# The second feed-forward product of a fused graph layer, computed in two halves of 128 output columns

## The chip, the cores and the metric

The kernel runs on one core of one Trainium2 chip. The metric is the device time of one execution in microseconds. The profile is one execution taken by the hardware profiler; its times are counted from the start of its span.

## The reference

There are 64 graphs of 256 nodes with 256 features, all in 32-bit floats. Each graph goes through two layers of attention over an adjacency matrix. The part that matters here is the end of the first layer: a layer normalisation, a feed-forward block with 1024 hidden columns, and a second normalisation.

```
x  = _ln(src + attn_out, g1, beta1)                 # [256, 256] for one graph
ff = gelu(x @ W1 + b1, approximate=False) @ W2 + b2 # [256, 1024] @ [1024, 256]
x  = _ln(x + ff, g2, beta2)
```

The second product, `gelu(...) @ W2`, is the one that is changed.

## The kernel before

One graph is a program of some hundred operations, written by `program(g)`. Each operation names its engine, what it reads and what it writes. The function `in_order` sorts the operations of all 64 graphs by a due time: the graph's number times `PERIOD` (50.00) plus the entry of the operation in `STARTS`. The first four graphs and some at the end have lists of their own, `FIRST` and `LAST`. The due times set only the order in which each engine takes its instructions; semaphores do the rest. Work of several graphs is so interleaved that TensorE always finds a matmul of some graph whose inputs are ready.

The work of one graph on TensorE, by the names in the profile, is: `pq`, `pk`, `pva` (projections), `s` (scores, four heads side by side in 32 rows each), `po` (attention times values, four heads side by side in 32 columns each), `pwo`, then `ph` (`x @ W1`, line 717), `pw` (the product with W2, line 735; also `pwo`, `pwa`, `pwb` of line 364 are matrix products of the same size of tile), and the projections of the second layer. In the first two and the last three graphs TensorE also makes transposes `py` and `po` at line 412; elsewhere these are made by another way.

The hidden activations `hT` lie as eight chunks of 128 hidden columns on the partitions, each with 256 nodes. For the second product, `emit_w2` takes for each half `t` of the nodes the eight chunks in turn: a 128x128 piece of `hT` is the stationary operand (loaded as weights) and the chunk of `w2` with all its 256 output columns is the moving operand. Eight matmuls add up in one half of the PSUM tile `pw2`; there are 16 for a graph. Four operations of two matmuls each are written per half `t`. A 32-bit matmul leaves two records of a weight load and two of a matmul in the trace, so a graph shows 32 of each at line 735 and the whole kernel 2048.

After `pw2` is complete, VectorE adds the residual in place (`add_dve`, line 442), takes statistics, normalises into `y1`, and hands on to the second layer.

Of the kernel before, what the change touches and what calls it, by code (L numbers as in the profile page):

```python
# [23 lines left out]
P = 128  # L24
# [21 lines left out]
def in_order(programs, starts, period, first, last):  # L46
# [4 lines left out]
    for g, p in enumerate(programs):  # L51
# [61 lines left out]
    "pw2#4": 140.62, "pw2#5": 141.02, "pw2#6": 141.41, "pw2#7": 148.05, "pw2#8": 148.44, "pw2#9": 148.83,  # L113
    "mv1": 151.17, "rs1": 152.34, "y1": 152.73, "y1b": 153.12, "x2": 157.03, "y1d": 160.16, "y1r": 160.55,
    "y1T": 165.62, "pk1": 168.36, "pq1": 169.92, "k1": 173.05, "q1": 175.39, "s100": 176.17, "e10/0": 179.30,
    "m10/1": 179.69, "e10/1": 180.08, "x2#2": 180.47, "m10/0": 181.64, "s110": 182.42, "m11/1": 182.81,
    "e10/1#2": 183.59, "m11/0": 186.33, "e11/0": 186.72, "pv1": 187.50, "v1": 187.89, "pwb": 188.28,
    "e11/1": 189.06, "e10/0#2": 191.80, "e11/0#2": 192.19, "e11/0#3": 193.75, "e11/1#2": 194.92, "e10/1#3": 195.31,
    "es11/0": 196.88, "zb": 197.27, "es10/1": 199.22, "e11/1#3": 200.00, "e10/0#3": 200.39, "es11/1": 200.78,
    "es10/0": 203.52, "po11": 204.69, "rd11": 205.08, "DVE:po11": 205.86, "po10": 207.81, "rd10": 208.20,  # L120
    "o1/1": 208.59, "o1/0": 212.50, "o1b": 212.89, "DVE:po10": 214.84, "pwa": 220.70, "o1d": 221.48, "o1r": 221.88,
    "mv2": 224.61, "rs2": 225.00, "pwa#2": 225.78, "mv3": 226.56, "rs3": 230.86, "y2": 231.25, "y2#2": 234.77,
    "y2#3": 235.16, "SP:y2": 245.70,
# [3 lines left out]
        -15695.655, -15149.395, -14793.414, -14575.593, -14576.679, -12389.4, -12473.121, -12768.633, -12325.705,  # L127
        -12962.633, -13646.112, -13920.766, -15032.506, -13982.705, -12245.782, -14367.9, -13407.27, -13364.314,
        -12295.865, -12278.788, -15117.887, -14534.961, -14147.504, -13724.315, -11168.884, -13648.66, -14956.242,
        -13925.311, -14243.822, -12844.486, -12674.163, -12439.242, -12618.202, -11646.197, -12711.361, -12646.602,  # L130
        -12660.005, -12483.679, -12536.223, -12670.679, -12672.041, -12540.947, -12616.664, -11428.13, -11287.329,
        -10559.998, -11327.61, -12104.073, -11981.91, -11451.573, -11390.504, -11925.878, -11920.644, -11949.974,
        -11934.31, -11218.912, -10721.604, -10477.164, -10272.81, -9911.323, -10046.084, -10003.332, -10003.33,
        -9888.664, -9828.572, -9137.591, -9093.292, -9361.474, -8629.104, -8880.603, -8662.925, -8385.643, -7361.835,
        -8390.399, -7992.367, -8899.947, -8751.386, -5428.043, -5165.028, -4818.157, -4818.155, -4676.943, -4605.749,
        -4416.199, -4343.259, -4285.804, -4281.04, -4239.384, -4213.9, -4213.898, -4184.711, -4179.417, -4120.528,
        -4116.71, -3848.303, -4082.576, -3952.079, -2701.19, -2573.78, -3544.133, -3351.674, -3835.864, -3735.264,
        -3368.002, -3295.807, -3198.79, -2449.601, -3771.22, -3786.52, -3591.972, -3579.658, -3043.106, -1795.518,
        -1513.493, -1500.436, -1651.414, -3219.503, -3097.003, -3058.447, -2754.345, -2674.088, -2325.015, -2665.857,
        -2767.649, -2502.329, -2296.094, -2078.474, -1848.912, -1820.665, -1784.337, -1810.803, -1497.873, -1460.302,  # L140
        -1376.277, -1486.102, -1312.035, -1183.27, -1105.604, -874.684, -688.763, -640.73, -479.139,
# [3 lines left out]
        -10275.79, -10222.682, -9516.48, -9944.344, -9446.908, -10225.155, -10205.062, -10225.153, -8955.48,  # L145
        -10029.465, -10140.425, -10210.028, -9873.068, -9835.535, -7377.261, -7180.288, -6824.629, -6777.573,
        -9204.865, -8944.093, -8767.724, -8328.16, -8466.442, -9151.761, -8929.815, -8096.162, -7584.68, -6703.905,
        -6451.399, -6098.908, -6444.96, -5961.777, -5877.676, -5160.502, -5109.467, -5086.245, -4692.889, -4420.43,
        -4163.756, -3604.27, -4281.353, -4268.9, -4351.895, -4326.041, -4245.629, -4209.422, -4083.279, -3835.868,
        -2477.164, -2455.124, -2262.278, -2252.074, -2126.011, -2126.009, -2085.054, -2084.485, -2082.849, -2082.237,  # L150
        -2003.412, -1980.986, -1933.415, -1872.594, -1896.355, -1270.113, -1738.724, -1639.29, -1717.421, -1448.705,
        -776.375, -412.725, -842.647, -287.979, -1280.266, -1198.698, -1128.404, -879.237, 70.142, 87.941, -1136.295,
        -1072.342, -1027.743, -460.056, -179.507, 204.948, 210.505, 214.846, 206.412, -1047.223, -408.661, -642.116,
        -358.078, -181.938, -6.862, 30.096, -722.148, 194.821, 209.783, 217.042, 218.303, 226.289, 226.571, 225.524,
        231.48, 237.007, 256.247, 254.861, 257.812, 257.814, 258.162, 258.552, 259.758, 267.688, 288.409,
    ],
    [
        -6647.961, -6937.505, -7329.132, -7090.883, -7287.519, -6750.27, -6499.303, -6250.569, -6335.205, -6198.913,
        -4279.455, -4146.698, -4153.953, -4099.89, -5252.176, -4800.331, -4823.206, -3892.413, -4287.653, -5235.477,
        -4590.983, -4178.05, -5112.062, -3844.17, -3597.583, -3566.893, -3768.04, -4350.565, -4222.211, -4264.419,  # L160
        -4242.206, -3964.02, -4253.173, -4122.444, -4100.627, -4124.943, -3655.64, -3398.956, -3375.271, -3623.161,
        -3199.162, -2900.972, -2887.075, -2770.539, -2607.594, -2602.901, -2418.216, -2218.326, -2198.868, -2082.801,
        -1408.588, -2023.294, -1984.958, -2089.338, -2021.294, -1995.304, -1910.877, -1467.289, -1186.368, -333.252,
        -267.616, -156.633, 7.424, 76.774, 123.113, 123.368, 139.873, 149.02, 149.022, 149.024, 149.026, 159.236,
        168.958, 168.96, 168.962, 222.92, 287.196, 168.964, 170.479, 171.914, 173.278, 205.329, 207.947, 216.563,
        216.861, 176.494, 177.744, 178.409, 187.359, 208.634, 208.636, 180.981, 177.968, 180.983, 202.563, 202.565,
        208.638, 210.695, 212.315, 212.986, 181.086, 197.943, 188.886, 202.77, 209.238, 210.706, 194.919, 188.65,
        208.636, 208.638, 211.76, 218.917, 222.164, 222.166, 219.427, 223.473, 223.475, 233.005, 233.712, 233.714,
        233.362, 238.879, 243.498, 247.259, 248.724, 262.721, 289.372, 289.374,
    ],  # L170
    [
        -3461.383, -4284.528, -4612.308, -2804.152, -2140.617, -2122.888, -3258.861, -2978.606, -3119.93, -2972.723,
        -2165.719, -2120.695, -3398.916, -3131.95, -2419.282, -2394.817, -2186.356, -1899.734, -1900.194, -2312.452,
        -2003.4, -1753.187, -1779.463, -1249.761, -944.255, -944.079, -1047.498, -1911.55, -1631.466, -1637.536,
        -1299.479, -1521.291, -1834.945, -1597.607, -1397.96, -1539.304, -1196.6, -726.368, -580.763, -925.785,
        -509.463, -334.77, -263.148, -168.005, 59.328, 85.165, 104.993, 105.438, 108.842, 124.159, 143.944, 114.717,
        116.225, 124.453, 131.56, 146.986, 151.077, 133.857, 141.768, 155.476, 157.111, 158.347, 158.349, 158.351,
        158.353, 158.355, 158.357, 158.359, 159.116, 160.017, 160.115, 166.361, 167.109, 167.489, 168.742, 198.814,
        212.043, 169.653, 171.471, 169.448, 170.399, 204.058, 205.83, 182.958, 193.225, 175.454, 175.456, 178.467,
        187.187, 190.053, 191.779, 175.456, 178.907, 185.152, 200.986, 202.931, 210.134, 210.136, 211.221, 210.28,  # L180
        179.858, 188.999, 196.052, 198.766, 201.471, 204.23, 186.917, 189.993, 190.152, 198.004, 198.313, 210.696,
        211.816, 211.98, 210.698, 212.107, 220.203, 223.572, 224.434, 224.499, 221.504, 228.418, 228.42, 228.869,
        230.221, 257.27, 257.272, 263.277,
# [3 lines left out]
    [  # L187
        23.519, 13.207, 1.964, 57.459, 95.091, 64.105, 53.036, 55.397, 49.54, 52.235, 66.882, 69.681, 63.952, 67.444,
        63.253, 63.255, 67.027, 67.029, 64.134, 63.255, 63.255, 69.248, 68.931, 79.084, 85.684, 85.957, 87.538,
        67.348, 67.35, 69.834, 69.836, 72.036, 67.35, 72.729, 72.731, 78.757, 78.759, 85.365, 85.367, 85.396, 89.037,  # L190
        89.756, 89.769, 93.049, 96.238, 96.554, 106.07, 109.692, 109.694, 115.731, 126.316, 142.48, 143.083, 141.755,
        141.757, 116.193, 116.195, 111.062, 115.098, 150.04, 150.042, 150.753, 151.373, 151.375, 151.377, 151.59,
        151.592, 151.594, 153.406, 153.408, 153.41, 153.412, 156.132, 156.134, 162.974, 184.129, 313.3, 231.961,
# [47 lines left out]
def fast_path(nc, tc, a, out, bad):  # L241
# [11 lines left out]
    FC = FF // P  # L253

    with ExitStack() as ctx:
# [64 lines left out]
        def program(g):  # L320
# [4 lines left out]
            def T(name):  # L325
                return at_(g, name)
# [417 lines left out]
            y1r = turn("y1")  # L744
# [443 lines left out]
```

## Time and profile before

| | |
|---|---|
| time, median of 3 runs | 2811.23 us (2809.66 to 2811.77) |
| span of the profiled execution | 2809.7 us |
| TensorE matmul, busy | 2785.5 us, 21112 records |
| TensorE weight load, busy | 2090.4 us, 21112 records |
| VectorE / ScalarE / GpSimd, busy | 2070.7 / 1939.3 / 1988.5 us |
| second feed-forward product (line 735), busy | 453.4 us, 2048 records |
| mean granted TensorE clock | 0.997 |

The profile does not give the profiled execution's whole time apart from its span. The span equals the fastest of the three runs to 0.1 us, and the slowest is 2.1 us longer, so that is the room for what lies around it.

A row of the groups gives line, engine, operation, output and inputs, shape, count, then busy time in us and mean duration of one in ns. `PE` is the matmul side of TensorE and `PEld` its weight loads, which run beside the matmuls. [...] records of consecutive matmuls overlap: the pace of a stream is read from the time that a run of records takes in the chain or on the timeline, and not from the mean duration.

### The profile page before, as it was taken

How to read it: one execution, taken by the hardware profiler on the slowest of the kernel's cores; microseconds unless marked ns; L12 is line 12 of the kernel's file. 1: busy time of each engine (PE TensorE's matmuls, PEld its weight loads, DVE VectorE, ACT ScalarE, POOL GpSimd, SP SyncE). 2: the span in 40 equal slices, each digit the busy share in tenths (PEclk: the TensorE clock that was granted, in tenths of full speed). 3: DMA queues.
4: the chain of work that ended last, by engine and by line, in shares of the span. 5: the costliest groups of instructions: out<-in, count | busy, mean ns of one | idle time of the engine just before them, and what ended most of it. 6: DMA issues, size and time to landing. Idle time of an engine off the chain costs nothing.

```text
span 2809.7 us, 54277 instructions
## 1 busy us (share of the span) xinstructions
PE 2785.5 (99%) x21112; PEld 2090.4 (74%) x21112; DVE 2070.7 (74%) x3857; ACT 1939.3 (69%) x3131; POOL 1988.5 (71%) x1526
## 2 busy tenths in 40 slices
PE   9999999999999999999999999999999999999997
PEld 7777777777777777777777777777777777777775
DVE  5667777777777777777777777777777777777776
ACT  5766766767767667677676676776766767767663
POOL 3668767677676686776766867768668677677773
PEclk9999999999999999999999999999999999999999
DMA  3012222122222221212222212122222121221100
GB/s 132 23 47 68 59 70 61 53 72 58 60 68 58 64 61 53 75 58 58 68 61 61 63 52 76 57 58 69 60 61 65 50 76 58 56 83 48 53 27 13
DMA packets 269750, 169.55 MB, mean 60 GB/s; under 512 B 18608, under 2 KB 268976, under 8 KB 269488
## 3 DMA queue, kind: packets, MB, share of 16 engines
q1 hardware_dynamic: 269216, 165.76, 20.5%
q8 instruction: 169, 2.77, 0.4%
q14 instruction: 93, 0.76, 0.1%
q10 hardware_dynamic: 272, 0.26, 0.0%
HBM read 102.77 MB, written 63.18 MB: 59 GB/s over the span
## 4 chain that ended last, share of the span: by engine, by line
PE 97%; DVE 2%; ACT 0%; POOL 0%; issue 0%; DMA 0%; SPq 0%; DVEq 0%; POOLq 0%; ACTq 0%
PE ph L717 16%; PE pw L735 16%; PE po L524 12%; PE s L485 10%; PE pk L350 8%; PE pva L669 8%; PE pq L350 8%; PE pv L364 4%; PE po L531 4%; PE pwo L364 4%; PE pwa L364 4%; PE pwb L364 4%; DVE rd L540 1%; ACT e L501 0%; DVE e L510 0%
## 5 line engine op out<-in xcount | busy, mean ns | idle before, releaser
L558 POOL TENSOR_TENSOR es<-e 128x512 f32<-128x512 f32 x504 | 637.3, 1275 | 580.7 <-issue 441.3
L769 POOL TENSOR_TENSOR e<-e,m 128x1024 f32<-128x1024 f32 x252 | 595.2, 2374 | 105.0 <-DVE e L510 97.8
L540 DVE RECIPROCAL rd<-po 128x256 f32<-128x256 f32 x256 | 440.1, 1737 | 41.3 <-PE po L531 41.3
L717 PE MATMUL ph<-y0T,w 128*128 128x256 f32 x2048 | 466.7, 380 | 1.1 <-ACT y0T L431 0.7
L735 PE MATMUL pw<-w,hT 128*128 128x256 f32 x2048 | 453.4, 379 | 0.0
L717 PEld LDWEIGHTS ph<-y0T,w 128*128 128x128 f32 x2048 | 389.1, 191 | 83.0 <-issue 17.4
L501 ACT ACTIVATE e<-e 128x1024 f32<-128x1024 f32 x256 | 268.5, 1050 | 262.1 <-POOL e L769 261.2
L735 PEld LDWEIGHTS pw<-w,hT 128*128 128x128 f32 x2048 | 388.8, 190 | 53.8 <-issue 1.1
L510 DVE TENSOR_TENSOR m<-s,neg 128x1024 f32<-128x1024 f32 x256 | 311.0, 1216 | 109.0 <-ACT e L501 82.2
L501 ACT ACTIVATE e<-s 128x1024 f32<-128x1024 f32 x256 | 261.0, 1022 | 173.2 <-DVE m L510 96.1
L510 DVE TENSOR_TENSOR e<-s,neg 128x1024 f32<-128x1024 f32 x256 | 304.8, 1214 | 15.8 <-PE s L485 8.1
L765 ACT ACTIVATE m<-s 128x1024 f32<-128x1024 f32 x252 | 252.0, 1026 | 67.1 <-PE s L485 38.9
L485 PE MATMUL s<-q,k 32*128 32x256 f32 x4096 | 294.6, 400 | 0.7 <-ACT q L563 0.7
L485 PEld LDWEIGHTS s<-q,k 32*128 32x128 f32 x4096 | 185.5, 184 | 127.1 <-issue 51.9
L524 PE MATMUL po<-e,v 128*32 128x256 f32 x4096 | 271.9, 383 | 4.1 <-ACT v L563 3.0
L501 ACT ACTIVATE m<-m 128x1024 f32<-128x1024 f32 x256 | 265.3, 1069 | 1.6 <-DVE m L510 1.5
L461 POOL TENSOR_TENSOR rs<-ve,neg_half 128x2 f32<-128x2 f32 x256 | 179.9, 703 | 94.8 <-DVE ve L456 86.8
L669 PE MATMUL pva<-wv,xT 128*128 128x512 f32 x512 | 246.4, 604 | 0.4 <-PE s L485 0.4
L501 ACT ACT_TABLE_LOAD x127 | 162.9, 1283 | 87.9 <-PE s L485 86.7
L724 ACT ACTIVATE hT<-ph,cols 128x256 f32<-128x256 f32 x512 | 209.3, 476 | 20.4 <-PE ph L717 18.8
L677 DVE TENSOR_TENSOR v<-pva,rows 128x512 f32<-128x512 f32 x128 | 87.3, 683 | 170.3 <-PE pva L669 170.2
L524 PEld LDWEIGHTS po<-e,v 128*32 128x32 f32 x4096 | 119.9, 110 | 113.3 <-issue 41.8
(107 smaller groups left out, 4652.5 us busy)
## 6 DMA issues: line engine op xcount, KB each, us to landing
xT<-xT_dram SPq DMA_DIRECT2D x64, 256.0 KB, 3.2
x<-x_dram SPq DMA_DIRECT2D x64, 256.0 KB, 3.0
adj<-adjT_dram SPq DMA_DIRECT2D x64, 256.0 KB, 3.7
out_dram<-y SPq DMA_DIRECT2D x64, 256.0 KB, 2.2
y0d<-y0b SPq DMA_DIRECT2D x236, 64.0 KB, 1.8
y0r<-y0d SPq DMA_DIRECT2D x59, 256.0 KB, 2.8
y1d<-y1b SPq DMA_DIRECT2D x236, 64.0 KB, 1.8
y1r<-y1d SPq DMA_DIRECT2D x59, 256.0 KB, 2.8
```

Of the source, the lines that this page charges most:

```text
L350: nc.tensor.matmul(pt[:, o, :], lhsT=w[:, c, o * P : (o + 1) * P], rhs=s[:, c, :], start=(c == 0), stop=(c == KC - 1),)
L364: nc.tensor.matmul(pt[:, t, :], lhsT=T(s)[:, c, t * P : (t + 1) * P], rhs=w, start=(n == 0), stop=(n == len(parts) - 1),)
L485: nc.tensor.matmul(s[j // 2][:, j % 2, c, :], lhsT=kT[r, hg, c * P : (c + 1) * P], rhs=qT[r, hg, :], start=True, stop=True,)
L501: nc.scalar.activation(T(dst)[:, j], s, AF.Exp, scale=scale, **kw)
L510: lambda: nc.vector.tensor_tensor(T(dst)[:, j], T(src), T("neg")[:, None].to_broadcast([P, 2, NT, D]), ALU.add),
L524: nc.tensor.matmul(po[j * DH : (j + 1) * DH, 0, :], lhsT=v(c, j), rhs=T(e)[:, j, c, :], start=(n == 0 and c == 0), stop=(n == len(parts) - ...
L540: op("DVE", [po], [f"{rd}:rd"], lambda: nc.vector.reciprocal(T(rd), T(po)[:, 1, :]))
L558: lambda: on.tensor_tensor(T(dst)[:, j], T(e)[:, j, 0, :], T(e)[:, j, 1, :], ALU.add),
L669: nc.tensor.matmul(pv.rearrange("p r d -> p (r d)"), lhsT=s[:, c, t * P : (t + 1) * P], rhs=wv0[:, c].rearrange("p r d -> p (r d)"), start ...
L717: nc.tensor.matmul(ph[:, i, :], lhsT=w1[:, c, (f + i) * P : (f + i + 1) * P], rhs=s[:, c, :], start=(c == 0), stop=(c == KC - 1),)
L735: nc.tensor.matmul(T("pw2")[:, t, :], lhsT=T("hT")[:, f + i, t * P : (t + 1) * P], rhs=w2[:, f + i, :], start=(f + i == 0), stop=(f + i == ...
L769: nc.gpsimd.tensor_tensor(T(f"e1{hg}")[:, j], T(f"e1{hg}")[:, j], T(f"m1{hg}")[:, j], ALU.add)
```

## The change

Each half `t` of the second product is made in two halves `h` of 128 output columns. For each `h` the eight chunks of `hT` are taken again as weights, and the moving operand is half a chunk of `w2`, 128 columns. So 16 matmuls of 256 columns per graph become 32 of 128 columns. The same products are added in the same places of `pw2`. The due times get eight more entries per graph, which repeat neighbouring values.

```
             for t in range(NT):
-                for f in range(0, FC, 2):
-
-                    def emit_w2(t=t, f=f):
-                        for i in range(2):
-                            nc.tensor.matmul(
-                                T("pw2")[:, t, :], lhsT=T("hT")[:, f + i, t * P : (t + 1) * P], rhs=w2[:, f + i, :],
-                                start=(f + i == 0), stop=(f + i == FC - 1),
-                            )
-
-                    op("PE", [f"hT/{f}", "c_w2"], ["pw2:g"], emit_w2)
+                for h in range(2):
+                    for f in range(0, FC, 2):
+
+                        def emit_w2(t=t, f=f, m=slice(h * P, (h + 1) * P)):
+                            for i in range(2):
+                                nc.tensor.matmul(
+                                    T("pw2")[:, t, m], lhsT=T("hT")[:, f + i, t * P : (t + 1) * P], rhs=w2[:, f + i, m],
+                                    start=(f + i == 0), stop=(f + i == FC - 1),
+                                )
+
+                        op("PE", [f"hT/{f}", "c_w2"], ["pw2:g"], emit_w2)
...
-    "pw2#4": 140.62, "pw2#5": 141.02, "pw2#6": 141.41, "pw2#7": 148.05, "pw2#8": 148.44, "pw2#9": 148.83,
+    "pw2#4": 140.62, "pw2#5": 140.62, "pw2#6": 140.62, "pw2#7": 140.62, "pw2#8": 140.62, "pw2#9": 141.02,
+    "pw2#10": 141.41, "pw2#11": 148.05, "pw2#12": 148.44, "pw2#13": 148.44, "pw2#14": 148.44, "pw2#15": 148.44,
+    "pw2#16": 148.44, "pw2#17": 148.83, "mv1": 151.17, "rs1": 152.34, "y1": 152.73, "y1b": 153.12, "x2": 157.03,
...
```

The lists `FIRST` and `LAST` change in the same way.

## The prediction

> **What bounds the kernel now.** I read the busy shares first, then the chain of work that ended last, then the groups at line 735.
>
> ```profile
> PE 2785.5 (99%) x21112; PEld 2090.4 (74%) x21112; DVE 2070.7 (74%) x3857; ACT 1939.3 (69%) x3131; POOL 1988.5 (71%) x1526
> ...
> PE 97%; DVE 2%; ACT 0%; POOL 0%; issue 0%; DMA 0%; SPq 0%; DVEq 0%; POOLq 0%; ACTq 0%
> ...
> L735 PE MATMUL pw<-w,hT 128*128 128x256 f32 x2048 | 453.4, 379 | 0.0
> ...
> L735 PEld LDWEIGHTS pw<-w,hT 128*128 128x128 f32 x2048 | 388.8, 190 | 53.8 <-issue 1.1
> ```
>
> TensorE's matmul side is busy 99% of the span and makes up 97% of the chain, so what lengthens its stream lengthens the kernel. The list of waits shows no wait of TensorE at all between 500 and 2000 us. The changed product stands in that stream with no idle time before its matmuls (0.0). Its weight loads, 190 ns each, fit beside matmuls and still leave 53.8 us in which the loading side is idle: before, weights cost nothing here. The chain in order of time gives the pace:
>
> ```profile
> 1384.95 1.73 PE pwo L364 x8
> 1386.68 6.91 PE pw L735 x32
> 1393.59 0.43 PE pk L350 x2
> ```
>
> The 32 records of a graph take 6.91 us with nothing between them, 215.9 ns a record. The next graph's 32 begin at 1429.82, 43.14 us later, and so on through the steady part.
>
> [...] The `pva` records of 512 columns start 0.43 us apart,[...] when nothing runs before it, a 128x128 load lets its matmul start some 104 ns later (below), and in the steady part loads lie under the previous matmul. [...] the question is which ends last.
>
> **The change part by part.** Removed: 2048 records of 256 columns, 2048 x 215.9 ns = 442.2 us of PE stream. Added: 4096 records of 128 columns, each behind its own load. No semaphore wait is added: the only operand waited for is `hT`, as before, and the order of the other engines' instructions, POOL's and SP's queues included, is the same in the built kernel. On TensorE the 32 stay together where the 16 were; in graphs 0, 1 and a few at the ends they are cut at the same places or, with the repeated due times, a few matmuls later. VectorE's add at line 442 starts after the last `pw` record as before and so shifts with it; PE has no wait on it in the steady part, since everything behind it on PE shifts by the same amount. All that is to be priced is the pace of a 128-column record with its own load. The steady part of before has none; I bound it from three places.
>
> First, the matmul itself. The transposes at line 412 are 128-column 32-bit records, each with a load:
>
> ```profile
> 2797.10 0.42 PEld L412 LDWEIGHTS po<-ident,o 128*128 128x128 f32 x4
> 2797.10 0.66 PE L412 MATMUL po<-ident,o 128*128 128x128 f32 x4
> ```
>
> The first of such a run has a record of about 329 ns, as the longest of that line does; three more take 0.66 - 0.33 = 0.33 us, 109 to 110 ns each. [...] so the matmul side alone gives 4096 x 109.2 = 447.3 us, +5.1 us. Their loads, 140 ns long, are shorter than those of ordinary weights, so this is a lower bound: the loading side may be later, not earlier.
>
> Second, the nine warm-up matmuls of 128 columns with ordinary weights. [...]
>
> ```profile
> 3.91 1.06 PE L861 MATMUL warm<-mean_w,ones 128*128 128x128 f32 x4
> ```
>
> Each record there is 421 ns, so (1.06 - 0.421) / 3 = 213 ns a record[...], although a load's record there is 333 ns (median of the line). Loads do follow one another faster than their records are long; 190 ns is no pace, and 4096 x 190 is ruled out.
>
> Third, and deciding: ordinary 128x128 loads under a 128-column record at full clock. They occur where a normal matmul follows a transpose, here `pw` itself near 60.5 us:
>
> ```profile
> L412 PE MATMUL py<-ident,y 128*128 128x128 f32 x3 | 0.5, 273 | 0.0
> L735 PE MATMUL pw<-w,hT 128*128 128x256 f32 x1 | 0.4, 382 | 0.0
> ...
> L735 PEld LDWEIGHTS pw<-w,hT 128*128 128x128 f32 x2 | 0.3, 191 | 0.0
> ```
>
> The `pw` record begins 109 ns after the last transpose's and lasts 382 ns where 379 is usual, and the same 382 stands in all seven places of this kind that I looked up (`pw`, `ph`, `pwa`). I read the 3 ns as waiting for weights: begun 1 to 2 ns after the transpose's matmul, the load was ready about 110 ns later, 112 ns from matmul to matmul. A second reading supports it: an exposed first load of `ph`
>
> ```profile
> 35.88 0.30 PEld L717 LDWEIGHTS ph<-y0T,w 128*128 128x128 f32 x2 [0.89 <-ACT y0T L431]
> 35.88 0.48 PE L717 MATMUL ph<-y0T,w 128*128 128x256 f32 x1 [0.66 <-ACT y0T L431]
> ```
>
> holds its matmul for 483 - 379 = 104 ns and its own record (186 ns) ends some 80 ns after that matmul truly starts. A load under a running matmul ends 190 + 2 ns after that matmul's start; 80 ns earlier is 112. So I take 112 ns: 4096 x 112 = 458.8 us, +16.6 us. All of it lies on the path, because PE has nothing else in its way: 0.26 us more per graph.
>
> Below, I do not go under 109.2 by much, as PE's own transposes show it. Above, 113 (one ns of reading on each load) gives 462.8 us, +20.6.
>
> Issuing costs nothing I can find: the `s` records (64 in 4.3 us of a graph, as many loads) show PE taking an instruction every 34 ns, and the new stream needs one every 56. The instruction queue moves 2.77 MB, 0.4% of the DMA engines; 4096 more records of the 54277 add 8% to that.
>
> Against the profiled span, 2809.7 + 16.6 = 2826.3 us; the median of the runs is 1.5 us above that span, which gives 2827.8.
>
> **The rivals.** A: the loads bind at 112 ns, +16.6 us, 2827.8 (0.60, the forecast; with 111 to 113 as its own range, 2823.7 to 2831.9).
>
> B: the loads stay hidden, because the 3 ns belong to the switch from transposing to multiplying and not to the load. Then the matmul side alone decides, 109.2 ns, +5.1 us, 2816.3: 0.18%, not slower by what can be told. For it: [...] an exposed load is ready after 104 ns. Against it: in one place the load after a transpose began 8 ns late and the matmul waited 5 ns, not 3, which a fixed switch cost would not do. [...] Chance 0.13.
>
> C: in between. At the same seven places the next load starts 110 ns after the one before (two loads fill 0.30 us, and the second is 192 ns); if that is the loads' own pace, 4096 x 110 = 450.6 us, +8.4 us, 2819.6. Chance 0.18.
>
> D: [...] the granted clock gives way: at 116 ns, +32.9 us, 2844. The page shows PEclk at 9 in all slices, and nothing in the trace asks for it. Chance 0.06.
>
> E: faster. [...] The transposes speak against it. Chance 0.03. That the change does not do what it says is excluded by the built kernel, which has 32 matmuls of 128 columns at this place.
>
> **How the numbers follow.** About 0.2% (5.6 us) is what a measurement of this kernel can tell from no change. Slower by more: A, C and D, 0.84. Within: B, and the smaller part of E, 0.14. Faster: 0.02. The range reaches from just under B to just over 113 ns a record: 2815.5 to 2833.
>
> **What would show it.** In the profile after, line 744 should have 4096 records, the chain should show `pw` with 64 records in about 7.17 us (7.0 for B, 7.04 for C), the period of a graph should be 43.40 us, and the matmul records of `pw` should be longer than the 273 ns that a 128-column record takes without waiting, by some 3 ns. Weight loading should be near full under `pw`. A wait of PE on another engine in the steady part, or other lines that take more than before, would make the working wrong, not only its size.

## The result, and the profile after

The changed kernel takes 2828.65 us (median of 3 runs, 2827.53 to 2831.84) against 2811.23: ratio 1.0064, interval 1.0045 to 1.0084. That is 17.4 us slower, 0.8 us from the forecast. The profiled execution is the slowest of the three: 2831.84 us, with a span of 2830.0. So the whole time is 1.8 us above the span, and the profile stands 3.2 us above the median. This matters below. In every execution of these kernels for which both figures are known the difference is 1.7 to 1.9 us. The span of 2809.7 us before therefore belongs to an execution of about 2811.5 us, near the median; that it equals the fastest of the three runs is a coincidence.

The page of the kernel after, busy shares, chain and the two groups of the changed line (744 now):

```profile
PE 2801.9 (99%) x23160; PEld 2160.4 (76%) x23160; DVE 2071.4 (73%) x3857; ACT 1940.0 (69%) x3131; POOL 1988.8 (70%) x1526
...
PE 95%; DVE 2%; ACT 1%; DMA 1%; POOL 1%; issue 0%; SPq 0%; DVEq 0%; POOLq 0%; ACTq 0%
...
L744 PEld LDWEIGHTS pw<-w,hT 128*128 128x128 f32 x4096 | 467.7, 192 | 4.4 <-issue 1.1
...
L744 PE MATMUL pw<-w,hT 128*128 128x128 f32 x4096 | 468.6, 275 | 0.0
```

The loading side, which had 53.8 us of idle time before its loads of this product, has 4.4 now: under `pw` it is full. On the chain TensorE's share has fallen from 97 to 95%, and DMA, ScalarE and GpSimd show 1% each, which the pace of `pw` doesn't explain. The chain of the kernel after in order of time (start, length, what):

```profile
1391.73 1.73 PE pwo L372 x8
1393.46 7.14 PE pw L744 x64
1400.61 1.73 PE pk L358 x8
```

64 records take 7.14 us where 32 took 6.91, and the neighbours keep their 1.73 and stay without gaps. The next `pw` starts at 1436.84, 43.38 us later (43.14 before). The records of line 744 between 500 and 2000 us, duration in ns as least, median and longest:

```profile
L744 PEld LDWEIGHTS pw<-w,hT x2176: 190/192/192, 525.5 to 1964.1; 128*128 128x128 f32 x198
L744 PE MATMUL pw<-w,hT x2176: 272/275/275, 525.7 to 1964.2; 128*128 128x128 f32 x198
```

A 128-column record that doesn't wait is 272 to 273 ns long (the transposes before the change). Nearly all are 275: each waits some 2.5 ns. In the records' own starts, 2642 of the intervals inside `pw` are 112 ns and 1319 are 111, so the pace is 111.7 ns. The transposes before, whose loads are shorter (140 ns), follow one another after 109 ns (27 intervals) or 110 (8), 109.2 on the mean; I take that for the pace of a 128-column matmul alone.

Where the 20.3 us between the two spans lie follows from the starts of `pw` in both traces. Up to `pw` of graph 3: 180.32 against 180.26, +0.1. From there to `pw` of graph 60: 2470.92 against 2457.24, +13.7, which is 57 x 0.240. From there to the end: 178.75 against 172.20, +6.5, of which four graphs of 0.24 make 1.0. The prediction had no term for the other 5.5.

The +0.1 at the start is a sum of opposite parts. Three split products lie in it, 0.7 by the pace, but the profile before also has a stretch of 3.4 us at half clock (a granted clock of 0.50 from 36.7 to 40.1 us), which the profile after lacks. Such a stretch near 36 to 38 us comes in eight of the fourteen profiles of both kernels and all experiments, and `pw` of graph 3 starts anywhere between 178.3 and 182.7 us in the twelve profiles whose `pw` records keep one of the two paces above.

The longer end shows first as 2.9 us in which TensorE is idle, near 2680 us. Tiles that have to be transposed go out to memory in four transfers of 64 KB and come back turned. `o1d` is the outward one for the attention output of the second layer, `o1r` the way back, and `y1d` and `y0d` are outward ones of the same kind. In the first profile after, the last of four `o1d` lands 3.57 us after its issue; in the profile before it takes 1.8.

### The profile page after: what moved, and what is told of

Read it like the earlier page. It is cut to its first block, busy times and chain, and to the rows that moved or that the text cites. A ratio compares the mean times of both kernels' runs of the same rounds, so it can differ in the third digit from the quotient of the medians.

```text
span 2830.0 us, 58376 instructions
## 1 busy us (share of the span) xinstructions
PE 2801.9 (99%) x23160; PEld 2160.4 (76%) x23160; DVE 2071.4 (73%) x3857; ACT 1940.0 (69%) x3131; POOL 1988.8 (70%) x1526
## 3 DMA queue, kind: packets, MB, share of 16 engines
q1 hardware_dynamic: 269216, 165.76, 20.4%
q8 instruction: 185, 3.03, 0.5%
## 4 chain that ended last, share of the span: by engine, by line
PE 95%; DVE 2%; ACT 1%; DMA 1%; POOL 1%; issue 0%; SPq 0%; DVEq 0%; POOLq 0%; ACTq 0%
PE pw L744 16%; PE ph L725 15%; PE po L532 12%; PE s L493 9%; PE pk L358 8%; PE pva L677 8%; PE pq L358 8%; PE pv L372 4%; PE po L539 4%; PE pwo L372 4%; PE pwa L372 4%; PE pwb L372 4%; DVE rd L548 1%; ACT e L509 0%; POOL e L778 0%
## 5 line engine op out<-in xcount | busy, mean ns | idle before, releaser
L744 PEld LDWEIGHTS pw<-w,hT 128*128 128x128 f32 x4096 | 467.7, 192 | 4.4 <-issue 1.1
L744 PE MATMUL pw<-w,hT 128*128 128x128 f32 x4096 | 468.6, 275 | 0.0
L774 ACT ACTIVATE m<-s 128x1024 f32<-128x1024 f32 x252 | 251.8, 1025 | 68.4 <-PE s L493 38.8
L469 POOL TENSOR_TENSOR rs<-ve,neg_half 128x2 f32<-128x2 f32 x256 | 180.1, 703 | 111.7 <-DVE ve L464 104.4
```

Source lines behind the costliest of these rows:

```text
L744: nc.tensor.matmul(T("pw2")[:, t, m], lhsT=T("hT")[:, f + i, t * P : (t + 1) * P], rhs=w2[:, f + i, m], start=(f + i == 0), stop=(f + i == ...
```

## The experiments

Two questions are left: is it the weight load that sets 111.7 ns, and what lengthens the last four graphs. Theory and rival of each run are in its expectation. Times of one group stand beside the runs of before on the same chip.

**The changed kernel again** (`e0_after`, no edit).

> The changed kernel once more, to see which part of its first profile belongs to the change. Theory (a weight load under a 128-column matmul sets the pace, 111.7 ns a record): 64 graphs x (64 x 111.7 - 32 x 215.8 ns) = +15.5 us, so 2826 to 2828 us against a before of 2811, and a period of 43.38 us. The late landing of o1d near the end of the first profile (3.57 us, TensorE idle 2.9 us, then slow for some us) is chance: this profile should not have it, and its span should be about 2826. Rival: the end of the kernel is upset by the change itself, then the idle time of some 3 us before ph near 2680 us comes again in the same place.

2830.23 us (5 runs, 2828.08 to 2833.86) against 2810.19: 1.0077 (1.0063 to 1.0091). The period is 43.377 us again. The profile has no late `o1d`, and its span is 2826.3 as expected, but it is of the fastest of the five runs. The median is above the expectation, so the runs lose more than the pace explains.

**Quarters of 64 columns** (`e1_quarters`).

```
-  w2[:, f + i, :]      # 256 columns, 8 chunks
+  for at, width in cuts[n]:                     # (0,64), (64,64), (128,64), (192,64)
+      m = slice(at, at + width)
+      for f in range(FC):  ... T("pw2")[:, t, m] ... rhs=w2[:, f, m]
```

> The second product in four quarters of 64 columns, each with its own loads: 8192 records. Theory (load sets the pace): [...] the load keeps 108 to 112 ns, so 128 records take 13.9 to 14.3 us a graph and the kernel gains 447 to 473 us: 3258 to 3285. Rival (the 111.7 ns are a matmul of 128 columns[...]): 58.3 ns a record, 477.6 us in all, +36 us: about 2847.

3283.64 us (2 runs) against 2810.19, +473: the load's pace. The chain of that kernel:

```profile
1361.99 14.24 PE pw L738 x128
...
1412.52 14.24 PE pw L738 x128
```

The columns per record are halved again and the interval stays at 111 to 112 ns, so the matmul's width has no part in it. The matmul of 64 columns alone is an estimate of some 56 ns: the paces of 256 and 128 columns, 215.8 and 109.2, are 106.6 apart, and half of that comes off 109.2. The rival's 58 ns a record come from 111.7 in the same way; its 36 us are excluded. The load also keeps 111.7 ns under that short matmul, and does not fall to the 108 ns after which the next load follows an exposed one (35.880 and 35.988 us in the trace before). A limit on how fast TensorE takes instructions is no explanation either: the `s` records, each with a load of its own, follow one another every 67 ns on the mean in the same trace (16 in 1.08 us).

**192 and 64 columns in turn** (`e2_192_64`).

```
+  for m in (slice(0, 192), slice(192, 256)):
+      nc.tensor.matmul(T("pw2")[:, t, m], ..., rhs=w2[:, f + i, m], start=True, stop=True)
```

> Pieces of 192 and of 64 columns in turn, so as many records and columns as in the changed kernel; nothing is accumulated (each matmul overwrites), so that the output is only that of the last chunk. Theory (a load starts only when the matmul before it starts, and takes some 110 ns): 162.5 ns after a 192-column record, 111.7 ns after a 64-column one, 64 records in 8.77 us a graph, +1.87 us a graph, +119 us: about 2930. Rival (loads run further ahead and average out over wide and narrow records): 111.7 ns on the mean, +15 us: about 2827.

2932.52 us (2 runs) against 2810.19, +122. The chain of that kernel, and its matmuls between 500 and 2000 us by shape (busy us, mean ns):

```profile
1353.75 8.72 PE pw L736 x64
1398.75 8.72 PE pw L736 x64
```

```profile
L736 PE MATMUL pw<-w,hT 128*128 128x192 f32 x1083 | 293.0, 352 | 0.0
L736 PE MATMUL pw<-w,hT 128*128 128x64 f32 x1084 | 179.3, 247 | 0.0
```

As many records and columns as in the changed kernel cost 45.00 us a graph, +1.87, as worked out. A record that waits for weights begins before its columns move (382 ns long instead of 326 for a wide one, 275 instead of 219 for a narrow one), so the pace is taken from the ends, each less the length without a wait. It is 162 or 163 ns after a wide record and 111 or 112 after a narrow one. Nothing averages out. In the trace each load starts within 2 ns of the moment at which the matmul before it truly starts (in the profile after, 1 to 3 ns after the start of a record that waits some 2.5), so every record here costs the longer of its matmul (162.5 ns for 192 columns, midway between 109.2 and 215.8, an estimate) and the next one's load (111.7).

**The two halves of a chunk in direct succession** (`e3_inner`): the loop over halves inside the loop over chunks, `start=True, stop=True`.

> Halves of 128 columns, with the two halves of a chunk one after the other, so that the same piece of hT is wanted twice in a row; nothing is accumulated (each matmul overwrites), so that the output is only that of the last chunk. Theory: each matmul still brings its own two loads, so the pace is that of the changed kernel, 111.7 ns, and the time 2826 to 2829. Rival: weights wanted twice in a row are loaded once; then half the records have no load, the pace falls to the matmul's 109.2 ns or between, and the time to about 2816 to 2821.

2828.93 us (5 runs) against 2810.19: 1.0069 (1.0055 to 1.0083), period 43.377 us, again 4096 loads. The order of the halves saves no load. As the pace is that of the changed kernel, overwriting instead of accumulating, as here and in `e2_192_64`, does not alter it.

**The first product in halves instead** (`e4_ph_halves`; `pw` whole).

```
+  for m in (slice(0, P), slice(P, 2 * P)):
       for c in range(KC):
-          nc.tensor.matmul(ph[:, i, :], lhsT=w1[...], rhs=s[:, c, :], ...)
+          nc.tensor.matmul(ph[:, i, m], lhsT=w1[...], rhs=s[:, c, m], ...)
```

> The kernel before with the first product (ph, line 717) split into halves of 128 moving columns instead of the second; pw stays whole. Theory: the rule is one of record width and load and not of this product, so 4096 records at 111.7 ns take the place of 2048 at 215.8: +240 ns a graph (period 43.38 us), +15.4 us in all, 2825 to 2829 where before is 2810 to 2811. The exposed loads ahead of ph stay as they are. Rival: ph has slack that pw has not (its matmuls wait for y0T or follow exposed loads), then the gain in time is under 8 us.

2827.74 us (5 runs) against 2811.12: 1.0061 (1.0047 to 1.0075), +16.6. Its chain:

```profile
1394.56 6.91 PE pw L736 x32
1410.64 5.36 PE ph L718 x48
1424.17 1.78 PE ph L718 x16
```

The same groups in the kernel before:

```profile
1359.62 5.18 PE ph L717 x24
...
1372.97 1.73 PE ph L717 x8
```

Before, 24 records of `ph` took 5.18 us and 8 took 1.73; now 48 take 5.36 and 16 take 1.78, +0.23 in all, and `pw` is back at 6.91. With +0.24 for `pw` in halves, the price belongs to the shape and not to the product.

**Further profiles of both kernels, for the end** (`e5_before_look1`, `e6_before_look2`, `e7_after_look`; no edits).

> The kernel before, one more look, for the landing of the last o1d transfers before the tail. If a late landing (3.5 us instead of 1.8) is chance, it shows here too in some looks, with TensorE idle 2.5 to 3 us ahead of ph; if the change brings it, TensorE is idle 0.5 us at most ahead of ph, as in the first profile of before.

> The kernel before, a further look, for the same question: a landing of o1d of 3.5 us near 2656 us in a look at before makes it chance.

> The changed kernel, a third look, for the same question: with a late landing of o1d near 2670 us the span should be about 2830, without one about 2826; the period stays 43.377 us in both.

Before: spans of 2807.6 and 2806.9 us, no late `o1d` in this place, 171.7 and 171.3 us from `pw` of graph 60 to the end. One graph earlier an `o1d` does take 3.7 and 3.3 us in them, but TensorE doesn't wait for it. After: `o1d` in time, and yet a span of 2829.4 and 178.2 us to the end. TensorE waits 2.2 us for VectorE's `v` further on (0.9 in the first profile before) and then runs 3.4 us at half clock: 16 `po` records of one kind take 1.70 us from 2733.03 us on and 0.87 from 2736.49 on. My expectation, one late transfer or a span of 2826, was too narrow.

**Halves in the first 60 graphs only, and in the last four only** (`e8_split_first60`, `e9_split_last4`).

```
+  split = g < 60        # e9_split_last4: g >= 60
   def emit_w2(..., m=slice(h * P, (h + 1) * P) if split else slice(0, D), n=2 if split or h == 0 else 0)
```

> The second product in halves for graphs 0 to 59 only; the last four graphs keep the 16 wide matmuls. The pace theory gives 60 x 0.24 = +14.4 us. If the split in the last graphs is what makes the end longer, the stretch from the start of pw of graph 60 to the end of the span is again 171 to 172 us as before, and the time is 2824 to 2826. If the longer end is chance or comes from elsewhere, that stretch is 174 to 179 us and the time 2827 to 2831.

> The reverse: halves in graphs 60 to 63 only. The pace theory gives 4 x 0.24 = +1.0 us, 2811 to 2812. If the split in the last graphs makes the end longer, the stretch from pw of graph 60 to the end is 174 to 179 us and the time is 2813 to 2817. If not, it is 172 to 173 us and the time within 1.5 us of before.

First 60: 2827.11 us (5 runs, 2824.46 to 2828.39) against 2809.9, 1.0058 (1.0044 to 1.0071), and 173.5 us from `pw` of graph 60 to the end. The stretch lies between the two expectations, the time in the range of the second. Last four: 2816.26 us (21 runs) against the same, 1.0021 (1.0015 to 1.0028), and 178.2 us. Splitting four of 64 graphs, worth 1.0 us by the pace, costs 6.4: the end is longer because of the split there. The two costs, 17.2 and 6.4, add up to more than the 17.4 to 20.0 of the whole change, but within its intervals, so it can't be told whether the ends simply add.

The trace shows what happens in one of the two places. TensorE on the timeline of the kernel with the last four split:

```profile
2663.76 1.89 PE L358 MATMUL pq<-y1T,wq 128*128 128x256 f32 x8
2668.49 5.45 PE L725 MATMUL ph<-y0T,w 128*128 128x256 f32 x24 [2.84 <-DVE y L475]
```

In the kernel before the same wait is short:

```profile
2666.65 5.45 PE L717 MATMUL ph<-y0T,w 128*128 128x256 f32 x24 [0.49 <-DVE y L467]
```

`y` hangs on the chain `po`, `rd`, `o1`, then out to memory (`o1d`) and back (`o1r`). This is `o1d` in the DMA view of that kernel, and then of `e0_after`, each between the last issue and the landing. The line of GB/s cuts that time into 40 slices; `q8` is a DMA queue that carries instructions:

```profile
GB/s 120 192 192 121 39 120 186 181 170 44 88 170 181 345 50 0 0 0 0 0 0 0 0 0 0 0 0 0 5 5 11 11 11 0 0 0 0 0 0 0
...
q1 hardware_dynamic: 425, 0.19, 21.0%
q8 instruction: 1, 0.02, 2.5%
issues: line engine op xcount, KB each, median us to landing
o1d<-o1b SPq DMA_DIRECT2D x1, 64.0 KB, 3.7
```

```profile
GB/s 115 150 207 184 184 173 184 139 46 46 46 81 138 219 196 173 173 196 139 81 35 23 127 150 196 207 173 184 161 150 69 35 0 0 0 0 0 0 0 0
...
q1 hardware_dynamic: 428, 0.19, 44.6%
issues: line engine op xcount, KB each, median us to landing
o1d<-o1b SPq DMA_DIRECT2D x1, 64.0 KB, 1.8
```

The same bytes land after 3.7 or 1.8 us, and where they are late an instruction packet lies among them. In the first profiles before and after, every packet of `q8` has 16384 bytes (they take 0.9 to 1.8 us), and the whole kernel has 169 of them before and 185 after: 16 more for the 4096 added records of TensorE, one for every 256. The other engines' records are as many as before, so I read `q8` as fetching TensorE's instructions.

The packets in the trace show how the delay comes about. Of the 128 packets of 512 bytes that make up the late `o1d`, the last eight start only when the instruction packet ends, to within 20 ns, and then go one after another. This is so in all four profiles in which this `o1d` takes 3.46 to 3.74 us (first profile after, `e2_192_64`, `e3_inner`, `e9_split_last4`). Eight of 128 is a sixteenth, and the profile counts 16 DMA engines. That the fetch holds up the one on which it lies would fit this and is not shown: the traces do not name the engine. In the other four profiles with the last graphs split, the fetch starts after the last packet of `o1d` (by 0.1 us in `e7_after_look`) or lies elsewhere, and `o1d` takes 1.8 us. In the profiles without a split of `pw` there, none is late in this place.

The kernel before has such delays too. Of its 708 transfers of 64 KB under these three names, 25 take more than 2.9 us, and each of these has a packet of `q8` in its time; of the 628 without one none is that late (the longest takes 2.57). Fourteen of the 25 lie between 500 and 2000 us, where TensorE waits for nothing: there the transfers have slack.

What the split changes is where the fetches fall. Before, this fetch begins 25 to 30 us after the start of `pw` of graph 60. A split `pw` adds 64 instructions. The 60 graphs ahead add 3840, which is 15 fetches of 256 exactly, so they leave the places of the later ones nearly as they were (30.3 us in `e8_split_first60`). The split `pw` of graph 60 itself moves the fetch to 19.9 to 20.6 us (21.5 in `e2_192_64`, where all is later), and `o1d` is under way from about 18.6 to 20.4.

**The fetch moved by the warm-up** (`e10_before_shifted`, `e11_after_shifted`).

```
-  for _ in range(9):   # 128x128 warm-up matmuls
+  for _ in range(4):
+      ...
+  for _ in range(21):  # e11_after_shifted: 29
+      nc.tensor.matmul(warm[:1, 0, :1], lhsT=ones[:, :1], rhs=mean_w[:, :1], start=True, stop=True)
```

> The kernel before with pw whole; only its warm-up differs: 4 wide matmuls instead of 9 and 21 of one column, so that TensorE's stream is 64 instructions longer ahead of everything, as one split pw makes it ahead of the tail. Instruction fetch theory (a fetch of 16 KB, which comes at another place because the stream is longer, lies in the way of the last o1d transfers): the fetch that is 25 to 30 us after the start of pw of graph 60 before comes at 19 to 21 us, o1d lands after 3.5 us instead of 1.8, the stretch from pw of graph 60 to the end is 174 to 178 us instead of 171 to 172, and the time 2812 to 2817. Rival (it is the length of pw in the last graphs that sets off the longer end): the stretch stays 171 to 173 us and the time within 2 us of before.

> The changed kernel, all pw in halves, with 4 wide and 29 one-column matmuls as warm-up: 96 instructions more ahead of everything, so that the fetch at 20 us after pw of graph 60 comes some 8 to 10 us earlier. Instruction fetch theory: o1d lands after 1.8 us, the stretch to the end is 173 to 174 us, and the time 2825 to 2827, below the changed kernel's 2828 to 2830. Rival: the stretch stays at 174 to 179 us, and the time at 2828 to 2830.

With `pw` whole and only the stream shifted, the kernel before takes 2815.04 us (13 runs) against 2810.59: 1.0015 (1.0006 to 1.0023). The runs fall into two heaps, three at 2809 to 2811 and ten at 2814 to 2817. So instructions that do nothing for the result cost 4.5 us on the median, where the split in the last four graphs cost 6.4. The profile fell on a run of the lower heap: its fetch begins 20.4 us after `pw` of graph 60, 0.2 us after `o1d` has landed, and the stretch to the end is 171.9 us. No profile of the upper heap exists. That its 4 us are a late `o1d` is likely and not shown; they could also lie at the start, which the warm-up touches, or on another transfer.

The changed kernel with the shift takes 2829.95 us (5 runs): no gain, the expectation missed. Its stretch to the end is 174.1 us and `o1d` takes 1.8 us, as wanted. But the start is 2.4 us later than in the first profile after (`pw` of graph 3 at 182.68 us), the latest of all profiles. Why is not shown; with the other altered warm-up (`e10_before_shifted`) it is at 178.94. And the fetch, now at 13.3 us, sits on another transfer. SP's queue and TensorE in that kernel:

```profile
2665.92 3.08 SPq L401 DMA_DIRECT2D y1d<-y1b  x4
```

```profile
2674.06 2.05 PE L372 MATMUL pv<-wv,y1T 128*128 128x256 f32 x8 [1.37 <-ACT y1T L439]
```

The four issues of `y1d` take 3.08 us there and 1.78 in the first profile after. No version beat the kernel before.

## Why the prediction was right, and where it was off

**The bound.** Right: TensorE is the only thing in the way of the steady part. The added time per graph comes through undiminished, the streams of TensorE's other lines keep their pace, and between 500 and 2000 us the profile after shows no wait of TensorE on another engine (busy 1500.00 of 1500.00 us).

**The pace of a record.** Right in kind: the loads bind, A and not B. `e1_quarters` shows it, where a pace set by the matmul would by the rival's estimate have been 437 us faster. Off in size by a little: 111.7 ns where I took 112. Over 4096 records that is 1.2 us; with the old pace at 215.8 and not 215.9 (903 intervals of 216 ns and 182 of 215 between 500 and 2000 us), the pace makes 64 x 0.240 = +15.4 us where the sum had 16.6. Of the two readings of the same place, the one by the record's end (load end less 80 ns) held, and the one by the interval of the loads (C, 110 ns) fell. In that place the second load's record is 192 ns long and not 190, so it probably began a little before its place; the interval was no pace.

**Loads lie under the previous matmul.** Right as far as it went, and sharper than I had it: under that one alone. Otherwise `e2_192_64` would have averaged out to 111.7 ns, where it shows 162 or 163 and 111 or 112 in turn.

**Nothing else is moved.** Wrong, and this is the step that failed: "Issuing costs nothing I can find", with the instruction queue dismissed at 0.4% of the DMA engines. The count was nearly right (8% forecast; 2.77 MB became 3.03, 9%), the argument from a share was not. In the steady part a fetch collides with transfers that have slack; in the last four graphs the round trip of `o1` and `y1` through memory is on the chain, and a fetch that falls on it costs 1.8 us, which TensorE sees as an idle time of 2.9 us:

```profile
2669.89 3.57 DMA o1d<-o1b
2673.48 0.03 SPq L407
2673.54 3.01 DMA o1r<-o1d
2682.64 7.13 PE ph L725 x24
```

This is the chain of the first profile after. `ph` takes 7.13 us for 24 records where 5.45 are usual in this place: after the idle time the granted clock is 0.64 from 2682.6 to 2686.1. So 2.4 us of added idle and 1.7 of slow matmuls turn one late packet into 4 us. The slow clock doesn't always follow: `e9_split_last4` has the same idle time and 5.45 us for `ph`.

The rest of the longer end is explained only in part. Some of it is scatter of the clock and not of the split. From TensorE's wait of 2.1 us for VectorE's `o` it is 38.8 us to the end in `e0_after`, whose last graphs are split, and 40.2 in `e8_split_first60`, whose last graphs are whole; the second has one stretch of 3.4 us at half clock more.

The prediction's 16.6 and the measured 17.4 to 20.0 thus agree partly by luck: the pace gives 15.4, and start and end add 2 to 5 us that the sum left out. The range held both. Rival D, 116 ns a record, is excluded by the pace of 111.7; the granted clock between 500 and 2000 us is 1.00, and the intervals within `pw` there are 111 or 112 ns but for some thirty of 109 or 110.

## What to carry to other kernels

On a TensorE-bound kernel like this one, price a matmul as the longer of its own columns and the next one's weight load, record by record; wide records lent no time to narrow ones here (162 and 112 ns in turn). With 32-bit 128x128 weights the load set 111.7 ns in these runs, so 128 moving columns (109.2) were just too few to hide it and 64 (some 56, an estimate) far too few. And count instructions as traffic: where a round trip through memory is exposed, a 16 KB fetch that falls on it delayed a transfer by 1.8 us here and TensorE by 2.4, and 64 more instructions ahead of it were enough to move it there. The fetches' small share of the DMA engines' time, 0.4% before and 0.5% after, said nothing about this.

## What I had not expected of the hardware

The load is not faster under a short matmul: 111.7 ns under one of some 56 ns (the estimate for `e1_quarters`) and under one of 109 ns alike, although the first load of `ph` after idle time, at 35.88 us before, lets its matmul start after 104 ns. Why a load under a matmul takes a few ns more stays open. And a single instruction packet of 16 KB, 1.2 to 1.5 us long, doubles the landing time of a transfer of 64 KB from 1.8 to 3.5 to 3.7 us while nearly all of the DMA engines are idle (their busy share is 0.02 from 2671.4 to 2673.4 us in the first profile after): eight of the transfer's 128 packets wait for it to end, and nothing else moves in the meantime (2671.32 to 2672.36 us there).
